# An attention and feed-forward block on one core: softmax rows turned in blocks of 32 on VectorE and carried by plain transfers, with the first rows, the second entry's blocks and the last rows in another order

## The chip, the cores and the metric

The kernel runs on one core of a Trainium2 chip. The metric is the device time of one execution in microseconds (us), given as the median of several runs. The profile is of one further execution. The engines are TensorE (PE for matmuls, PEld for weight loads), VectorE (DVE), ScalarE (ACT), GpSimd (POOL) and SyncE (SP), which here issues every transfer.

## What is computed

`x` has 2 entries of 1024 rows of 512. There are 16 heads of width 128, and the feed-forward part has 1365 hidden columns. Cut to what matters:

```python
xn = layernorm(x)
q, k, v = (einsum('bsd,hed->bhse', xn, W) for W in (W_Q, W_K, W_V))
scores = where(causal, -1e9, einsum('bhse,bhme->bhsm', q, k) / sqrt(128))
z = einsum('bhsm,bhme->bhse', softmax(scores), v)
x = x + layernorm(einsum('bhse,hde->bsd', z, W_O))
h1, h3 = (einsum('bsd,hd->bsh', layernorm(x), ternary(w)) for w in (w1, w3))
x = x + layernorm(einsum('bsh,dh->bsd', silu(h1) * h3, ternary(w2)))
```

`ternary(w)` rounds w/s to -1, 0 or 1 and multiplies by s, the mean of |w|.

## The kernel before

**Number forms.** A projection is made of three matmul products: a tensor is split into a lead and a low part and a difference of the two (`lead_and_low` L403, `difference_form` L412, for weights; `block_unit` L357 for x), in a 32-bit form[...]. `combine` (L423) puts the main and the difference product together. Scores (L522) and values (L584) are plain f32 matmuls, each of two instructions.

**Heads and steps.** N = 32 heads (16 for each of the two entries, b), two to a pair g. A head n has 8 rows i of 128 queries; row i has L = 128(i + 1) keys. `order` lists the 256 (n, i), and the loop at L683 takes one a step, idx. `scores(n, i)` (L517) does the row's matmuls into one of two `s_ps` buffers; DVE masks (L527) and takes the row maximum (L531), ACT makes exp and the row sum (L538), DVE inverts it (L543), ACT scales (L544). `look(idx + 3)` at step idx keeps the scores three rows ahead.

**Turning the softmax.** `values` needs the softmax with keys on the partitions. POOL copies the row's upper and lower 16-bit words apart (`half`, L549), SP issues one transposing transfer for the row (`halfT`, L554), and one step later `join` (L564) has DVE put the words together in `pt` (L570). Two rows share a `pt`, so a head has four pairs m, and `values(n, m)` (L575) multiplies 2m + 2 key tiles of 128x256. It runs where (idx - 3) is odd, for the pair that ended at idx - 3. ACT takes the result out twice (L593, L595), DVE and POOL make low and difference (L598, L601).

**What fills a step.** `put` gives steps of a head their extra matmul work: query and key projections of the next head (`query_key_unit` L432), values of the next pair of heads (`value_unit` L454), output projections of the last pair (`output_units` L478, each with two DVE operations L496 and L499 on `acc`). `side` holds small things by step: mean of |w|, statistics of the second entry, ternary weights (L187). Four `ps_m` buffers take the projection results.

**What sets the order.** A scheduler at compile time orders instructions in the order of the code and by readiness. `tc.issue_after(ins)` puts the instructions of a block behind `ins` on its own engine; `behind("max", "half", "exp", "turn")` (L508) does that with the last recorded row maximum (DVE), word copy (POOL), exp (ACT) and transposing transfer (SP). SP issues in order, and at most eight of its transfers are in flight, for they take turns on eight semaphores.

**First rows (L606 to L635).** x is loaded in eight tiles of 128 rows to `acc`, weights between. Statistics of rows 0 to 3 are taken, then `block_unit(0, t)` normalises on ACT (L366), transposes on PE (L375) and makes lead (ACT), low (DVE) and difference (POOL); rows 4 to 7's statistics are taken between. Queries and keys for the first 512 tokens follow, then the blocks of rows 4 to 7, queries and keys for the second 512, and then the loop at L677 with scores of three rows and four value units.

**Second entry's blocks (L705).** The eight `block_unit(1, t)` lie in steps 4 to 7 of head 14, each with its own load of x just ahead of its normalising.

**Last rows.** After the loop the last output units, values and join are mixed (L765 to L774). The feed-forward part then runs four blocks of 512 rows. In the last one `finish_last` (L833) does, for each row tile by itself: statistics from PSUM, root on ACT, three one-column DVE steps, output on ACT, the sum with `acc` on POOL (DVE for the last), and the store.

Of the kernel before, what the change touches and what calls it, by code (L numbers as in the profile page):

```python
# [28 lines left out]
P = 128  # L29
# [6 lines left out]
def sandwich_kernel(  # L36
# [67 lines left out]
    def row_stats(mv, src):  # L104
        st = small.tile([P, nc.vector.BN_STATS_DIM], FP, name="bnst")
        nc.vector.bn_stats(out=st, in_=src)  # L106
        nc.vector.bn_aggr(out=mv, in_=st)

# [209 lines left out]
    with ExitStack() as att:  # L318
        ppool = att.enter_context(tc.tile_pool(name="p", bufs=1))
        hpool = att.enter_context(tc.tile_pool(name="half", bufs=1))  # L320
        htpool = att.enter_context(tc.tile_pool(name="halfT", bufs=1))
# [9 lines left out]
        xs, r_in, shifts, lows_in, leads_in = {}, {}, {}, [], []  # L331
# [24 lines left out]

        def block_unit(b, t):  # L357
# [3 lines left out]
            if b == 0:  # L361
                src = xt = acc[:, t, :]
            else:
                src = xt = xpool.tile([P, D], FP, name="xt")
                nc.sync.dma_start(xt, x[b, ts(t, P), :])
            nc.scalar.activation(  # L366
                xt, src, AF.Identity, scale=r_in[b][:, t : t + 1],
                bias=shifts[b][:, t : t + 1],
            )
# [4 lines left out]
            for c in range(NC):  # L374
                nc.tensor.transpose(ps[:, c, :], xt[:, ts(c, P)], ident)  # L375
            lead, low, diff = (form[:, :, ts(tl, P)] for form in xs[b, k])
            leads_in.append(nc.scalar.mul(lead, ps, LEAD / T12).ins)  # L377
            lows_in.append(
                nc.vector.scalar_tensor_tensor(  # L379
                    low, lead, -T12, ps, ALU.mult, ALU.add  # L380
                ).ins
            )
            nc.gpsimd.tensor_tensor(diff, lead, low, ALU.subtract)
# [19 lines left out]
        def lead_and_low(kind, n, part):  # L403

            if (kind, n) not in weights:
                weights[kind, n] = [form(kind, "a"), form(kind, "l")]
            lead, low = (w[:, part] for w in weights[kind, n][:2])
            raw = wraw[kind, n][:, part]
            nc.scalar.mul(lead, raw, LEAD)
            nc.gpsimd.tensor_tensor(low, raw, lead, ALU.subtract)  # L410
# [21 lines left out]
        def query_key_unit(n, kind, k):  # L432
# [12 lines left out]
            for c in range(NC):  # L445
                nc.tensor.matmul(  # L446
                    diff, lhsT=forms[2][0][:, c, :], rhs=forms[2][1][:, c, :],
                    start=(c == 0), stop=(c == NC - 1),
                )
            combine(  # L450
                proj[n, kind, k], main, diff, SCALE if kind == 0 else 1.0
            )
# [64 lines left out]
        def scores(n, i):  # L517
# [27 lines left out]

            words = p_sb.bitcast(U16).rearrange("p (k two) -> p k two", two=2)
            half = hpool.tile([P, 2 * longest], U16, name=f"half{i % 2}")
            for k in range(2):
                copy = nc.gpsimd.tensor_copy(half[:, ds(k * L, L)], words[:, :L, k])  # L549
            marks["half"].append(copy.ins)  # L550
            halfT = htpool.tile(
                [P, 2 * (i % QT + QT + 1), P], U16, name=f"halfT{i % QT}"
            )
            turn = nc.sync.dma_start_transpose(  # L554
                halfT[:, 0 : 2 * (i + 1), :], half[:, : 2 * L]
            )
            marks["turn"].append(turn.ins)
            return halfT
# [5 lines left out]
        def join(n, i):  # L564
            turned = live.pop((n, i))
            m, il = divmod(i, 2)
            if il == 0:
                pts[n, m] = ptpool.tile([P, NT - 2 + 2 * (m % 2), KB], FP, name=f"pt{m % 2}")
            words = pts[n, m].bitcast(U16).rearrange("p t (q k) -> p k t q", k=2)
            nc.vector.tensor_copy(  # L570
                words[:, :, 0 : i + 1, ts(il, P)],
                turned[:, 0 : 2 * (i + 1), :].rearrange("p (k t) q -> p k t q", k=2),
            )

        def values(n, m):  # L575
# [5 lines left out]
            ps = ps_m.tile([P, TB], FP, name="mm")  # L581
            for kt in range(2 * m + 2):
                c0 = max(0, kt - 2 * m) * P
                nc.tensor.matmul(  # L584
                    ps[:, c0:KB],
                    lhsT=proj[g, 2][:, kt, ts(j, P)],
                    rhs=pts[n, m][:, kt, c0:KB],
                    start=(kt == 0),
                    stop=(kt == 2 * m + 1),
                )  # L590

            lead, low, diff = (w[:, ts(half, KB)] for w in zs[g, qb, j])
            nc.scalar.mul(lead, ps[:, :KB], LEAD / T12)  # L593
            copy = zpool.tile([P, KB], FP, name="zf", bufs=2)
            nc.scalar.copy(copy, ps[:, :KB])  # L595
# [12 lines left out]
        load_raw(0, 0)  # L608
        load_raw(1, 0)
        for t in range(QT, NT):  # L610
            stats_load(0, t)
        load_raw(2, 0)
        for t in range(NT):
            with ExitStack() as order:
                if t >= QT:
                    block_unit(0, t - QT)
                    order.enter_context(tc.issue_after(lows_in[t - QT]))
                row_stats(mv_in[0][:, t, :], acc[:, t, :])
                if t % 2 == 1:
                    std_unit(0, t - 1, 2)  # L620
            k = t - QT - 2
            if k >= 0:
                with tc.issue_after(lows_in[k + 1]), tc.issue_after(leads_in[k + 1]):
                    lead_and_low(k, 0, EVERY)
                    difference_form(k, 0, EVERY)
        for k in range(2):
            for t in range(QT, NT):
                if k == 1:
                    block_unit(0, t)
            for kind in range(2):  # L630
                query_key_unit(0, kind, k)
# [305 lines left out]
```

## Time and profile before

| | |
|---|---|
| median of 3 runs | 1545.23 us (1544.26 to 1546.73) |
| profiled execution, own time | 1546.35 us |
| its span | 1544.5 us |
| mean granted TensorE clock | 0.995 |
| instructions | 21108 |
| transfers by the first queue | 357512 packets, 163.62 MB, 47.2% of 16 engines |
| first matmul starts, last ends | 8.76 us, 1534.40 us |

The span is the time from the first to the last instruction that the profiler recorded; the execution's own time has 1.85 us around it. "Busy" counts an engine's instructions; a matmul's end is modelled, so PE's share is not its share of peak. A row of groups has line, engine, operation, tiles (written, then read), shapes and count, then busy us, mean ns of one, and idle time just ahead of them with what ended it. A row of waits has us in total, times and longest. Windows are counted from the start of the span.

### The profile page before, as it was taken

Reading aid. Unit: us, or ns where it says so; the run is one execution under the profiler, and the core shown is the slowest. Engines: PE = TensorE matmul, PEld = TensorE weight load, DVE = VectorE, ACT = ScalarE, POOL = GpSimd, SP = SyncE. Lnnn points to the kernel's source line nnn. Section 1 sums busy time; section 2 is a strip of 40 time slices with the busy share of each in tenths; the row PEclk is TensorE's granted clock in tenths of the full one; section 3 lists DMA queues with packets and bytes.
Section 4 is the critical chain, followed back from the end, with each engine's and each line's share of the span. In section 5 each row is a group of like instructions: output and inputs, shape, how many; then the busy total and the mean of one; then the engine's idle time right before and its main releaser. Section 6 shows DMA issues by size and latency. Waiting matters only on the chain.

```text
span 1544.5 us, 21108 instructions
## 1 busy us (share of the span) xinstructions
PE 1488.7 (96%) x7078; PEld 1188.7 (77%) x7078; DVE 1165.4 (75%) x2101; ACT 789.2 (51%) x1568; POOL 790.5 (51%) x861
## 2 busy tenths in 40 slices
PE   5999999999999999999999999999999999999997
PEld 4777878787878786876787877777878877788885
DVE  5678787878787879798888888888887786455343
ACT  4555545454556455556655555555555564344233
POOL 4465555555555667767766666666665441210010
PEclk9999999999999999999999999999999999999999
DMA  2465555555554456457655555555554457210000
GB/s 88 82 143 122 111 122 108 122 110 121 109 130 96 107 112 140 114 116 166 163 117 116 116 117 116 117 117 116 109 103 89 81 125 213 86 55 7 35 28 28
DMA packets 357622, 164.97 MB, mean 107 GB/s; under 512 B 311093, under 2 KB 324405, under 8 KB 357513
## 3 DMA queue, kind: packets, MB, share of 16 engines
q1 hardware_dynamic: 357512, 163.62, 47.2%
q8 instruction: 56, 0.92, 0.2%
q14 instruction: 54, 0.43, 0.1%
HBM read 73.39 MB, written 14.68 MB: 57 GB/s over the span
## 4 chain that ended last, share of the span: by engine, by line
PE 47%; DVE 4%; issue 1%; POOL 1%; ACT 1%; DMA 1%; SPq 0%; ACTq 0%; DVEq 0%; POOLq 0%
PE mm L298 10%; PE mm L584 8%; PE mm L441 6%; PE s_ps L522 6%; PE mm L465 5%; PE yp L806 5%; PE mm L485 4%; PE mm L446 3%; DVE pt L570 1%; DVE nm L531 1%; PE trx L238 0%; DVE bnst L106 0%; POOL half L549 0%; DVE raw L208 0%; POOL acc L266 0%
## 5 line engine op out<-in xcount | busy, mean ns | idle before, releaser
L549 POOL COPY half<-p_sb 128x640 uint16<-128x640 uint16 (+7 forms) x512 | 348.9, 711 | 436.7 <-issue 301.5
L538 ACT ACTIVATE p_sb<-s_ps,nm 128x128 f32<-128x128 f32 (+7 forms) x256 | 190.1, 743 | 351.0 <-DVE nm L531 328.7
L522 PE MATMUL s_ps<-k,q 128*128 128x512 f32 (+3 forms) x768 | 289.6, 486 | 1.9 <-ACT p_sb L538 1.8
L584 PE MATMUL mm<-pt,v_sb 128*128 128x256 f32 (+1 forms) x1280 | 271.6, 359 | 8.5 <-DVE acc L496 5.8
L584 PEld LDWEIGHTS mm<-pt,v_sb 128*128 128x128 f32 x1280 | 238.9, 190 | 51.5 <-DVE acc L496 13.3
L570 DVE COPY pt<-halfT 128x256 uint16<-128x256 uint16 (+7 forms) x256 | 272.6, 1065 | 0.5 <-DMA halfT<-half 0.5
L544 ACT ACTIVATE p_sb<-p_sb,ri 128x128 f32<-128x128 f32 (+7 forms) x256 | 198.4, 775 | 118.9 <-DVE ri L543 118.2
L531 DVE TENSOR_REDUCE nm<-s_ps 128x1 f32<-128x128 f32 (+7 forms) x256 | 193.2, 755 | 6.1
L601 POOL TENSOR_TENSOR zd<-za,zl 128x256 fp32r<-128x256 f32 x128 | 148.6, 1161 | 74.9 <-DVE zl L598 74.9
L522 PEld LDWEIGHTS s_ps<-k,q 128*128 128x128 f32 x768 | 130.6, 190 | 65.5 <-issue 54.7
L465 PE MATMUL mm<-va,xb 128*128 128x256 f32 x512 | 153.1, 299 | 2.2 <-DVE k L426 2.2
L527 DVE TENSOR_TENSOR s_ps<-s_ps,causal 128x128 f32<-128x128 f32 x256 | 75.0, 293 | 94.3 <-PE s_ps L522 93.2
L465 PE MATMUL mm<-vd,xb 128*128 128x256 f32 x512 | 144.7, 284 | 1.4 <-ACT k L424 1.4
L465 PE MATMUL mm<-vl,xb 128*128 128x256 f32 x512 | 144.4, 282 | 0.0
L441 PE MATMUL mm<-xb,qa 128*128 128x512 f32 x256 | 121.0, 473 | 1.4 <-ACT xb L377 1.4
L441 PE MATMUL mm<-xb,ka 128*128 128x512 f32 x256 | 113.1, 442 | 0.1
L441 PE MATMUL mm<-xb,ql 128*128 128x512 f32 x256 | 102.8, 402 | 2.5 <-DVE xb L379 2.5
L465 PEld LDWEIGHTS mm<-va,xb 128*128 128x128 f32 x512 | 97.7, 191 | 7.0 <-DVE k L426 2.6
L441 PE MATMUL mm<-xb,kl 128*128 128x512 f32 x256 | 101.9, 398 | 0.6 <-POOL kl L410 0.6
L465 PEld LDWEIGHTS mm<-vl,xb 128*128 128x128 f32 x512 | 97.8, 191 | 4.4 <-issue 2.4
L485 PE MATMUL mm<-oa,za 128*128 128x512 f32 x256 | 95.5, 454 | 4.8 <-DVE acc L496 3.5
L465 PEld LDWEIGHTS mm<-vd,xb 128*128 128x128 f32 x512 | 97.4, 191 | 2.2 <-ACT k L424 1.6
(150 smaller groups left out, 2815.8 us busy)
## 6 DMA issues: line engine op xcount, KB each, us to landing
wqk<-wq SPq DMA_DIRECT2D x32, 256.0 KB, 3.4
wqk<-wk SPq DMA_DIRECT2D x32, 256.0 KB, 3.6
wvo<-wv SPq DMA_DIRECT2D x16, 512.0 KB, 3.9
wvo<-wo SPq DMA_DIRECT2D x16, 512.0 KB, 3.8
xt<-x SPq DMA_DIRECT2D x32, 256.0 KB, 3.4
raw<-w SPq DMA_DIRECT2D x30, 256.0 KB, 3.4
tern<-raw SPq DMA_DIRECT2D x30, 256.0 KB, 2.7
xt<-w SPq DMA_DIRECT2D x24, 227.5 KB, 3.1
```

The lines of the kernel that those rows point to most:

```text
L298: nc.tensor.matmul(ps[:fl, :], lhsT=t[:, c, :], rhs=bl[k][:, c, :], start=(c == 0 and k == 0), stop=(c == NC - 1 and k == 1),)
L441: nc.tensor.matmul(main, lhsT=forms[f][0][:, c, :], rhs=forms[f][1][:, c, :], start=(c == 0 and f == 0), stop=(c == NC - 1 and f == 1),)
L465: nc.tensor.matmul((main, main, diff)[f][:, ts(t, 2 * P)], lhsT=forms[f][0][:, c, token], rhs=forms[f][1][:, c, :], start=(t == 0 and c == ...
L485: nc.tensor.matmul((main, main, diff)[f], lhsT=zs[g, t // QT, j][f][:, ts(t % QT, P)], rhs=weights[3, g][f][:, 2 * j : 2 * j + 2, :], star ...
L522: nc.tensor.matmul(s_ps[:, ds(k0, kl)], lhsT=proj[n, 0, i // QT][:, ts(i % QT, P)], rhs=proj[n, 1, k0 // TB][:, :kl], start=True, stop=True,)
L531: top = nc.vector.tensor_reduce(nm, s_ps[:, :L], axis=AX.X, op=ALU.max, negate=True)
L538: e = nc.scalar.activation(p_sb[:, :L], s_ps[:, :L], AF.Exp, bias=nm, accum_out=rs)
L544: nc.scalar.mul(p_sb[:, :L], p_sb[:, :L], ri)
L549: copy = nc.gpsimd.tensor_copy(half[:, ds(k * L, L)], words[:, :L, k])
L570: nc.vector.tensor_copy(words[:, :, 0 : i + 1, ts(il, P)], turned[:, 0 : 2 * (i + 1), :].rearrange("p (k t) q -> p k t q", k=2),)
L584: nc.tensor.matmul(ps[:, c0:KB], lhsT=proj[g, 2][:, kt, ts(j, P)], rhs=pts[n, m][:, kt, c0:KB], start=(kt == 0), stop=(kt == 2 * m + 1),)
L601: nc.gpsimd.tensor_tensor(diff, lead, low, ALU.subtract)
```

## The change

1. Softmax: a row goes from `scores` as it is. `turn(n, i)` has DVE transpose it in blocks of 32x32 into a tile `blocks`. The even row's missing key tile is cleared by POOL. When the odd row of a pair is done, SP issues 16 plain transfers, one for each source strip of 32 partitions and each destination strip, in runs of 64 words (256 B). `values` reads the last key tile and writes back in strips of 32. `half`, `halfT` and `join` go.
2. `turn(idx + 2)` is called at step idx, `values` at idx for the pair that ended at idx - 2, and output and value units lie in other steps.
3. The second entry's blocks lie one a step, from step 5 of head 14, with the load of x one step ahead.
4. First rows: a square root ahead of all; statistics and normalising in pairs of rows, odd rows normalised on DVE; wv loaded ahead of rows 4 to 7; first q and k leads on DVE; half of the differences on DVE; main products of q and k ahead of their difference products; value units between the second blocks and the queries and keys.
5. Last rows: all turned in the loop; `finish_last` works on pairs, with row 3 ahead of row 2 on DVE.

```diff
+    nc.scalar.activation(small.tile([P, 1], FP, name="root", bufs=1), eps, AF.Sqrt, bias=eps)
...
+        def block_load(b, t):
+            normal[b, t] = xt = xpool.tile([P, D], FP, name="xt")
+            nc.sync.dma_start(xt, x[b, ts(t, P), :])
+
+        def normal_unit(b, t):
+            if b == 0:
+                normal[b, t] = acc[:, t, :]
+            xt = normal[b, t]
+            if b == 0 and t % 2 == 1:
+                return normalise(xt, xt, mv_in[b], r_in[b], t)
+            return nc.scalar.activation(
+                xt, xt, AF.Identity, scale=r_in[b][:, t : t + 1],
+                bias=shifts[b][:, t : t + 1],
+            )
...
+            eng = nc.vector if b == 0 and tl >= QT // 2 else nc.gpsimd
...
-            words = p_sb.bitcast(U16).rearrange("p (k two) -> p k two", two=2)
-            half = hpool.tile([P, 2 * longest], U16, name=f"half{i % 2}")
-            for k in range(2):
-                copy = nc.gpsimd.tensor_copy(half[:, ds(k * L, L)], words[:, :L, k])
...
-            turn = nc.sync.dma_start_transpose(
-                halfT[:, 0 : 2 * (i + 1), :], half[:, : 2 * L]
-            )
...
+        def turn(n, i):
+            L = (i + 1) * P
+            p_sb = live.pop((n, i))
+            m, il = divmod(i, 2)
+            kts = 2 * m + 2
+            if il == 0:
+                blocks_of[n, m] = b = tpool.tile(
+                    [P, 4 * (NT - 2 + 2 * (m % 2)), 2, 32], FP, name=f"blocks{m % 2}"
+                )
+                clear = nc.gpsimd.memset(b[:, 4 * (kts - 1) : 4 * kts, 0, :], 0.0)
+                marks["half"] += 2 * [clear.ins]
+            b = blocks_of[n, m]
+            nc.vector.transpose(
+                b[:, 0 : 4 * (i + 1), il, :],
+                p_sb[:, :L].rearrange("p (b r) -> p b r", r=32),
+            )
+            if il == 0:
+                return
...
+            moved = b.rearrange("p (t b) i r -> p t b (i r)", b=4)
+            for to in range(4):
+                for of in range(4):
+                    move = nc.sync.dma_start(
+                        pt[ts(to, 32), 0:kts, ts(of, 64)], moved[ts(of, 32), 0:kts, to, :]
+                    )
+            marks["turn"] += 2 * [move.ins]
...
+        with past(*normal_pair(0)):
+            done = normal_pair(2)
+        with past(*done):
+            for kind in range(2):
+                lead_and_low(kind, 0, EVERY, first=True)
+            blocks = [block_unit(0, t) for t in range(QT)]
+        lead, low, diff = blocks[-1]
+        with past(diff):
+            for kind in range(2):
+                difference_form(kind, 0, EVERY)
+        for rest in [query_key_unit(0, kind, 0) for kind in range(2)]:
+            rest()
+        with past(lead, diff, blocks[1][2]):
+            for part in (FRONT, BACK):
+                lead_and_low(2, 0, part)
+                difference_form(2, 0, part)
+            done = normal_pair(4)
+            with past(*done):
+                normal_pair(6)
...
+        value_unit(0, 0)
+        for t in range(QT, NT):
+            block_unit(0, t)
+        value_unit(0, 1)
+        look(0)
+        for kind in range(2):
+            query_key_unit(0, kind, 1)()
+            look(1 + kind)
+            load_raw(kind, 1)
+        value_unit(0, 2)
+        for k in range(2):
+            turn(*order[k])
+        value_unit(0, 3)
...
-                put((0, 1, 1, 3, 5, 7, 7, 7), outs)
...
+                put((0, 0, 0, 2, 2, 4, 6, 6), outs)
...
-                if idx >= 3 and (idx - 3) % 2 == 1:
-                    rest = values((idx - 3) // NT, (idx - 3) % NT // 2)
+                if idx >= 2 and (idx - 2) % 2 == 1:
+                    rest = values((idx - 2) // NT, (idx - 2) % NT // 2)
...
-                if idx > 0:
+                if idx + 2 < len(order):
                     with behind("max"):
-                        join(*order[idx - 1])
+                        turn(*order[idx + 2])
...
+            for u in (t, t - 1) if t == QT - 1 else (t - 1, t):
+                y, yp, tt = last["y"][:, u, :], yps[b, tb][u], tb * QT + u
+                ua, ushift = last["a"][:, u : u + 1], last["shift"][:, u : u + 1]
+                if u == QT - 1:
+                    nc.vector.tensor_scalar(y, yp, ua, ushift, ALU.mult, ALU.add)
+                else:
+                    nc.scalar.activation(y, yp, AF.Identity, scale=ua, bias=ushift)
+                eng = nc.vector if u >= QT // 2 else nc.gpsimd
+                eng.tensor_tensor(y, y, acc[:, tt, :], ALU.add)
+                nc.sync.dma_start(out[b, ts(tt, P), :], y)
```

## The prediction

> **What bounds the kernel now.** I read the page's busy shares first, then its chain and its costliest groups, then the windows of 50 us and of 5 us, PE's waits, and last SP's own queue, since the change puts 2048 transfers on it.
>
> ```profile
> PE 1488.7 (96%) x7078; PEld 1188.7 (77%) x7078; DVE 1165.4 (75%) x2101; ACT 789.2 (51%) x1568; POOL 790.5 (51%) x861
> PE 47%; DVE 4%; issue 1%; POOL 1%; ACT 1%; DMA 1%; SPq 0%; ACTq 0%; DVEq 0%; POOLq 0%
> L549 POOL COPY half<-p_sb 128x640 uint16<-128x640 uint16 (+7 forms) x512 | 348.9, 711 | 436.7 <-issue 301.5
> L570 DVE COPY pt<-halfT 128x256 uint16<-128x256 uint16 (+7 forms) x256 | 272.6, 1065 | 0.5 <-DMA halfT<-half 0.5
> L531 DVE TENSOR_REDUCE nm<-s_ps 128x1 f32<-128x128 f32 (+7 forms) x256 | 193.2, 755 | 6.1
> ```
>
> PE bounds: it is idle for 1544.5 - 1488.7 = 55.8 us in all, and the change removes no matmul. So the work taken from POOL (L549) and DVE (L570) is worth only what it frees of those 55.8 us. The windows say where they lie (time, PE, PEld, DVE, ACT, POOL, clock, DMA share, GB/s):
>
> ```profile
> 0.00:50.00 50.00, 33.75 (x155) 27.08 (x156) 24.88 (x51) 22.23 (x41) 18.80 (x26) 0.93 0.23 78
> 600.00:650.00 50.00, 46.31 (x230) 36.24 (x230) 42.09 (x70) 30.31 (x60) 38.23 (x36) 1.00 0.59 138
> 700.00:750.00 50.00, 43.43 (x223) 34.09 (x222) 43.13 (x87) 33.16 (x60) 37.38 (x37) 1.00 0.75 186
> 1500.00:1550.00 50.00, 34.40 (x152) 27.52 (x150) 15.38 (x33) 13.40 (x21) 3.70 (x3) 0.92 0.06 21
> ```
>
> 16.3 us are idle in the first 50, 2.1 in the next 50, 22.2 over 100 to 1250 (summed over those windows; 3.7 and 6.6 in the two shown), 5.2 over 1250 to 1350, 10.1 behind the last matmul. PE's waits in the middle are nearly all for DVE:
>
> ```profile
> PE mm L584 <- DVE acc L496: 5.8, 8, 0.8
> PE mm L485 <- DVE acc L496: 3.5, 4, 1.3
> PE mm L446 <- DVE q L428: 2.8, 2, 1.5
> ```
>
> At the start there is a loss beside idle time. From 17.7 to 22.4 us the 128x512 matmuls start 0.43 us apart, later 0.23; from 30 to 39.6 again 0.43, with a granted clock of 0.69 and 0.66 in the rows 30:35 and 35:40. Those are about 11 and 18 matmuls at 0.2 us extra.
>
> **SP's queue, the resource that the change loads.** SP's timeline (start, us from first to last end):
>
> ```profile
> 0.72 1.82 SPq L335 DMA_DIRECT2D acc<-x  x4
> 3.53 1.89 SPq L335 DMA_DIRECT2D acc<-x  x4
> 576.40 0.57 SPq L213 DMA_DIRECT2D tern<-raw  x1
> 577.02 0.42 SPq L193 DMA_DIRECT2D raw<-w  x1
> 577.56 0.49 SPq L396 DMA_DIRECT2D wqk<-wk  x1
> ```
>
> A plain transfer issues in 0.43 us, and back to back the starts lie 0.46 to 0.48 us apart, 0.51 where it waits for one eight places earlier (4.48 to 5.00 us). L193 is the nearest in shape (512 pieces of 512 B): its own issue is 0.42, the next starts 0.54 after it.
>
> **The change, part by part.** It is summed against the profiled execution: 1546.35 us, span 1544.5, so 1.85 around it; the median shown, 1545.23, is 1.1 less.
>
> *Removed:* 512 POOL copies (348.9 us), 256 joins on DVE (272.6 us), 256 transposing transfers on SP (median issue 1.33 us, 341 us). None is on PE's path: at their ends PE waited 2.4 us for pt.
>
> *Added on DVE:* 256 block transposes of 128xL f32. No row shows one. Nearest is L531, the same 256 shapes read once: 0.755 us, 193 us; the upper end is the joins' own 1.065. Less than nothing is excluded, since they read every element. I take 0.755: DVE falls by 80 us, to 70%. On POOL 128 clears of 128x128 at 0.20 us (the ident memset at 0.71 us): 26 us, hidden, POOL being near 30%. These clears and the transposes now wait for moves that still read the blocks. Behind them on DVE stand the next mask and row maximum, for which ACT's exp and then PE wait. A block buffer comes round three steps after its moves were queued, 3 x 4.8 = 14.5 us; the moves need 16 x 0.5 + 3 = 11 us. Covered; every us beyond stands on PE's path.
>
> *Added on SP:* 128 pairs x 16 moves. With 0.47 to 0.54 us each a pair costs 7.6 to 8.6 us, and some 230 other transfers in the attention add 0.9. A pair has two steps: (1283 - 45)/128 = 9.67 us before, 9.6 with the gain below. So SP goes to 88 to 99%. I take 0.49, 91%: the plain back-to-back rows, since a move has 64 to 256 pieces, fewer than L193. The pair's moves are queued four steps (19 us) ahead of the matmuls that read them; they need 11. Below nothing: SP saves its 341 us of transposes, but nobody waited for SP, so no gain.
>
> *On the DMA engines:* 327,680 pieces of 256 B, 20,480 an engine. The packet records have 294,912 packets of 256 B (those of the transposes) at 22.8 ns in the mean and 10,240 plain ones of 512 B at 33.7. At 22.8 the pieces take 467 us an engine, at 33.7 690; with 250 us for the rest that is 58 to 76% of the 1229 us of attention. The Trainium skill speaks against it: "DMA: Bandwidth & Descriptors", section "Specifications", gives 512 B as the least size for line rate, with a read-modify-write below. If that doubled a packet of 33.7 ns, the pieces alone would take 1380 us, more than the stage, and the kernel would end near 1930 us. The same page, "Rules for kernel authors", puts a plain rearranging DMA at 19 times the hardware transpose: 19 x 3.6 us, the median landing of a transpose, is 68 us a row where a step has 4.8. I go with the rows. The trace moved 256 B packets as fast per packet as any, and here each run of 64 words is contiguous at both ends, the rearranging within 32 being DVE's.
>
> *Reads in strips of 32:* the last key tile's matmul has 128 columns as before (0.274 us) and ACT's two copies 256 (0.374, 0.367). If strips doubled ACT's, 256 x 0.37 = 95 us more put ACT at 57%: hidden, at nothing.
>
> *The middle.* values come a step earlier and the output units are spread over even steps; up to three still share a step. DVE, behind which PE waits, loses 0.31 us a step. Of 22.2 us idle I take 9 as gained; bounds 0 and 15. The second entry's x loads go one step earlier but on odd steps stand behind 16 moves (8 us, then 3.4 to land, against 4.8): ACT's normalising waits, exp and then PE behind it. Before, PE lost about 4 us there; I take the same, with 8 more as the upper end. Loads for normalising after attention meet the moves too: +2.
>
> *The start.* The early square root takes the table load (1.28 us at 5.47) into the wait for x (first statistics at 3.68). Two rows' statistics end at 5.4, root, reciprocal and shift at 6.2, the first transposes near 7.1 instead of 8.76. Rows 2 and 3 follow at 9.2; then DVE makes qa and ka (0.6 each, to 11.0) and four lows (0.69 each, to 13.8). The second matmul, which sat idle until low at 17.55, can go at 13.8: -3.7. From there 24 matmuls, at first slow, as before. Then the second half, 25.2 to 40.5 us: its 16 transposes and 24 matmuls are 7.2 us at full pace and two scores 0.3; the other 7.8 are 3.7 of idle on ACT, DVE and POOL and the slow clock. Value units (24 x 0.12 = 2.9 us each) now stand between; I leave 1.5 us: -6.3. DVE also has four rows' statistics and value forms in that stretch, so of -10 I take -8; bounds -4 and -11. Cover gone, each form that comes late costs its 0.7 to 1.3 us. wv goes ahead of rows 4 to 7 on SP (1.5 us later), needed only at 15 us.
>
> *The ends.* Of 5.2 us at 1250 to 1350 I take 1.5, as the last rows are turned two steps earlier. Behind the last matmul (1534.4) the last row's root waited on ACT to 1537.42 behind three outputs, and two tiny DVE steps took 0.74 and 1.18 beside POOL; its output issued at 1541.5. Now statistics end at 1535.4, root behind two outputs at 1536.6, three small steps to 1537.1, DVE 0.7 + 0.7, the other row's sum to 1539.3: -2.2, less POOL's interference, -2 (bounds 0 and -3).
>
> Sum: -8 - 9 + 2 - 1.5 - 2 = -18.5; on the median 1526.7, say 1527.
>
> **The rivals.**
> (1) SP becomes the bound. For: the 0.54 behind the many-piece transfer; only eight transfers are in flight. Against: 0.43 to 0.48 for plain ones. 2048 + 234 = 2282 issues fill 1229 us at 0.539 us each; above 0.547 the gain is used up, and it is slower. At 0.555 it costs 1266.5 - 1229 = 37.5: 1565 us.
> (2) The middle keeps its waits: the 22.2 us are the output units' turns, not DVE's load. Then only start and ends count, about -10: 1535.
> (3) The DMA engines bind by the 512 B rule: 1700 us or more. Against: the packet rows.
> (4) The change doesn't do what it says, the starts staying serial on DVE: part of (2), 1540 to 1546.
>
> **How the numbers follow.** Forecast 0.55 (1515 to 1538), rival (2) with (4) 0.16, of which 0.05 within 0.2%, rival (1) 0.25 (0.02 within), (3) 0.04. About 0.2% is what a measurement of this kernel can tell from no change. Faster 0.66, same 0.07, slower 0.27. The range 1513 to 1570 leaves out the worse half of (1), (3) and a small low tail; the forecast's own is 1515 to 1538.
>
> **What would show it.** Right: SP's move issues near 0.49 us with gaps between pairs; the DVE transpose near 0.75; PE idle in 100 to 1250 near 13; 128x512 matmuls at 0.23 us by 22 us; last output issued near 1539. Wrong: PE waiting for DMA pt, DVE's transpose waiting for DMA, SP's moves without gaps, 256 B packets over 40 ns.

## The result, and the profile after

The changed kernel takes 1865.7 us (median of 4 runs, 1865.4 to 1872.1) against 1544.7 before, measured again beside it: a ratio of 1.209, with an interval of 1.206 to 1.212. The forecast was 1527, its range 1513 to 1570; the result lies on the side of rival (1), at a price that rival (1) did not reach. The profiled execution took 1865.4 us, its span is 1863.6.

The page's busy shares, its chain, the group of block transposes and the largest moves (in the last line, the number is the time from issue to landing):

```profile
PE 1597.3 (86%) x7078; PEld 1233.2 (66%) x7078; DVE 1136.5 (61%) x2107; ACT 773.1 (41%) x1556; POOL 398.5 (21%) x472
...
SPq 40%; PE 28%; DMA 9%; issue 8%; DVE 8%; ACT 4%; POOL 3%; DVEq 0%; POOLq 0%; ACTq 0%
SPq L596 38%; PE mm L301 7%; PE mm L454 4%; DMA pt<-blocks 4%; PE yp L862 4%; PE s_ps L539 3%; PE mm L616 3%; PE mm L482 2%; PE mm L461 2%; PE mm L502 2%; ACT p_sb L555 1%; DVE blocks L584 1%; DVE acc L513 1%; DVE nm L548 1%; DMA raw<-w 1%
...
L584 DVE STREAM_TRANSPOSE blocks<-p_sb 128x128 f32<-128x128 f32 (+7 forms) x256 | 188.1, 760 | 78.6 <-DMA pt<-blocks 77.7
...
pt<-blocks SPq DMA_DIRECT2D x512, 64.0 KB, 2.2
```

The bound has moved. The chain that was PE's for 47% and SP's for 0% is now SP's for 40%, nearly all of it line 596, the moves. Every engine is less busy by share than before; nothing but SP's queue is full. The tile's own view gives least, median and most of one move's issue, and SP's timeline shows them in a row (start, us from first start to last end):

```profile
L596 SPq DMA_DIRECT2D pt<-blocks x2048: 585/601/1922, 38.2 to 1606.6; - x187
```

```profile
603.48 10.18 SPq L596 DMA_DIRECT2D pt<-blocks  x16
613.70 0.58 SPq L406 DMA_DIRECT2D wvo<-wv  x1
614.45 10.47 SPq L596 DMA_DIRECT2D pt<-blocks  x16
625.03 0.53 SPq L216 DMA_DIRECT2D tern<-raw  x1
625.60 0.43 SPq L196 DMA_DIRECT2D raw<-w  x1
```

Sixteen moves take 10.2 to 10.5 us, 0.64 to 0.66 a start. With the other transfers between, these pairs start 11.0 and 11.7 us apart (11.7 is also the median over the trace's records), where PE needs 9.6. There is no gap here: the next pair's moves are ready before SP is. The moves that carry 16 KB have nearly the same issue time as those that carry 64 KB (medians 0.595 to 0.609 us, worked out from the trace's records for the four sizes), so it is the count that costs.

Summed over the trace's records, SP's stretch with moves runs from 38.2 to 1607.2 us and holds 2282 transfers, as counted in the forecast. Their issues take 1379.3 us, the short gaps between them (under 0.3 us each) 121.9, together 1501.2 us or 0.658 us each; longer idle time is 67.8 us, of which 43 lie in 700 to 870. The forecast gave that stretch 1229 us. So 1501 - 1229 = 272 us is the price of an issue, and 68 is SP itself waiting. 1527 + 272 + 68 = 1867, against 1865.7 measured. This is bookkeeping, since SP's stretch is counted whole: that it closes says that the start and the ends came near the forecast. The experiments below test the causes.

What waits now, in the waits of the changed kernel (us in total, times, longest):

```profile
POOL blocks L581 <- DMA pt<-blocks: 434.7, 114, 12.1
ACT p_sb L555 <- DVE blocks L584: 363.3, 103, 9.4
...
PE mm L616 <- DMA pt<-blocks: 68.8, 30, 4.9
PE s_ps L539 <- ACT p_sb L555: 46.8, 31, 5.7
```

POOL's clears and DVE's transposes wait until moves have read the blocks, exp waits until a transpose has read its row, PE waits for exp and for the moves. The whole row hangs on SP from both sides.

The 68 us of idle SP is a second loss. In the stretch of the second entry's blocks the windows show PE at 69% of the time (time, PE, PEld, DVE, ACT, POOL, clock, DMA share, GB/s) and SP's timeline a period of 21 to 23 us for a pair:

```profile
700.00:870.00 170.00, 116.94 (x485) 88.98 (x484) 89.07 (x164) 62.79 (x123) 45.15 (x46) 0.84 0.37 87
```

```profile
755.67 10.18 SPq L596 DMA_DIRECT2D pt<-blocks  x16
765.94 1.01 SPq L363 DMA_DIRECT2D xt<-x  x2
767.00 0.42 SPq L406 DMA_DIRECT2D wvo<-wo  x1
778.30 10.25 SPq L596 DMA_DIRECT2D pt<-blocks  x16
```

The chain of waits in this stretch tells why SP stands still from 767.4 to 778.3, a stall that is as long as the moves themselves:

```profile
765.94 2.85 DMA xt<-x
768.82 0.82 ACT xt L371
769.69 1.11 PE tr L386 x4
770.80 4.18 PE mm L482 x24
774.98 3.26 PE mm L616 x16
```

The load of x (line 363) is queued behind the pair's 16 moves. ACT's normalising waits for it, PE's transposes wait for that, and the matmuls behind them on PE (value units, then the values whose end sets `pt` free) wait for PE. Only then can the next 16 moves start. It is a closed loop: moves, load, normalising, PE, moves.

### The profile page after: what moved, and what is told of

It reads as the page before. It is cut to its first block, busy times and chain, and to the rows that moved or that the text cites. A ratio compares the mean times of both kernels' runs of the same rounds, so it can differ in the third digit from the quotient of the medians.

```text
span 1863.6 us, 23761 instructions
## 1 busy us (share of the span) xinstructions
PE 1597.3 (86%) x7078; PEld 1233.2 (66%) x7078; DVE 1136.5 (61%) x2107; ACT 773.1 (41%) x1556; POOL 398.5 (21%) x472
## 4 chain that ended last, share of the span: by engine, by line
SPq 40%; PE 28%; DMA 9%; issue 8%; DVE 8%; ACT 4%; POOL 3%; DVEq 0%; POOLq 0%; ACTq 0%
SPq L596 38%; PE mm L301 7%; PE mm L454 4%; DMA pt<-blocks 4%; PE yp L862 4%; PE s_ps L539 3%; PE mm L616 3%; PE mm L482 2%; PE mm L461 2%; PE mm L502 2%; ACT p_sb L555 1%; DVE blocks L584 1%; DVE acc L513 1%; DVE nm L548 1%; DMA raw<-w 1%
## 5 line engine op out<-in xcount | busy, mean ns | idle before, releaser
L555 ACT ACTIVATE p_sb<-s_ps,nm 128x128 f32<-128x128 f32 (+7 forms) x256 | 188.5, 738 | 481.0 <-DVE blocks L584 363.3
L616 PE MATMUL mm<-pt,v_sb 128*128 128x256 f32 (+1 forms) x1280 | 294.9, 380 | 81.3 <-DMA pt<-blocks 68.8
L616 PEld LDWEIGHTS mm<-pt,v_sb 128*128 128x128 f32 x1280 | 252.7, 202 | 156.8 <-issue 94.2
L539 PE MATMUL s_ps<-k,q 128*128 128x512 f32 (+3 forms) x768 | 304.1, 517 | 48.3 <-ACT p_sb L555 46.8
L584 DVE STREAM_TRANSPOSE blocks<-p_sb 128x128 f32<-128x128 f32 (+7 forms) x256 | 188.1, 760 | 78.6 <-DMA pt<-blocks 77.7
L539 PEld LDWEIGHTS s_ps<-k,q 128*128 128x128 f32 x768 | 138.6, 198 | 136.5 <-issue 58.8
L636 POOL TENSOR_TENSOR zd<-za,zl 128x256 fp32r<-128x256 f32 x128 | 94.7, 740 | 471.3 <-DVE zl L633 435.2
L633 DVE SCALAR_TENSOR_TENSOR zl<-za,zf 128x256 fp32r<-128x256 f32 x128 | 68.6, 536 | 88.5 <-ACT zf L628 88.5
L581 POOL MEMSET blocks<- 128x128 f32 x128 | 26.1, 204 | 441.2 <-DMA pt<-blocks 434.7
L502 PE MATMUL mm<-od,zd 128*128 128x512 f32 x256 | 84.5, 411 | 39.5 <-ACT zf L628 37.8
L454 PE MATMUL mm<-xb,ql 128*128 128x512 f32 x256 | 113.9, 445 | 0.0
```

The source lines that it names most:

```text
L454: nc.tensor.matmul(main, lhsT=forms[f][0][:, c, :], rhs=forms[f][1][:, c, :], start=(c == 0 and f == 0), stop=(c == NC - 1 and f == 1),)
L502: nc.tensor.matmul((main, main, diff)[f], lhsT=zs[g, t // QT, j][f][:, ts(t % QT, P)], rhs=weights[3, g][f][:, 2 * j : 2 * j + 2, :], star ...
L539: nc.tensor.matmul(s_ps[:, ds(k0, kl)], lhsT=proj[n, 0, i // QT][:, ts(i % QT, P)], rhs=proj[n, 1, k0 // TB][:, :kl], start=True, stop=True,)
L555: e = nc.scalar.activation(p_sb[:, :L], s_ps[:, :L], AF.Exp, bias=nm, accum_out=rs)
L584: nc.vector.transpose(b[:, 0 : 4 * (i + 1), il, :], p_sb[:, :L].rearrange("p (b r) -> p b r", r=32),)
L616: nc.tensor.matmul(dst, lhsT=proj[g, 2][:, kt, ts(j, P)], rhs=rhs, start=(kt == 0), stop=(kt == 2 * m + 1),)
```

## The experiments

**What sets the price of a pair: the count of moves (first runs).** Two kernels were run beside the changed one: one with eight moves a pair, each of 128 words in place of 64, one with only the loads put ahead. The eight moves read the blocks of the first 64 partitions only, each twice, and leave out the rest, so they don't carry the whole softmax; they move the same number of bytes.

```diff
# eight moves (twice as wide)
-                for of in range(4):
+                for of in range(2):
-                        pt[ts(to, 32), 0:kts, ts(of, 64)], moved[ts(of, 32), 0:kts, to, :]
+                        pt[ts(to, 32), 0:kts, ts(of, P)], moved[ts(of, 32), 0:kts, ts(to % 2, P)]
# loads first: the load of x is queued on SP ahead of the step's moves
-            side[block_at - 1 + t].append(lambda t=t: block_load(1, t))
+            early[block_at - 1 + t] = t
...
+                if idx in early:
+                    block_load(1, early[idx])
                 if idx + 2 < len(order):
                     with behind("max"):
                         turn(*order[idx + 2])
```

> The changed kernel with 8 moves a pair instead of 16, each of 128-word runs instead of 64: the same bytes, half the issues; it fills pt with the right amount of data from the wrong strips, so the softmax is scrambled. Theory A (SP's issue of a move, 0.60 us and 0.04 between two, is the bound whatever the move's size): a pair falls from 16 x 0.64 + 0.95 = 11.2 to 6.1 us, below the 9.5 that PE needs, so PE is the bound again and the rest of the change shows: 1520 to 1540 us. Theory B (the bytes through the DMA engines, or the landing of a pair's data): the same bytes, so it stays above 1750 us.

Measured 1569.9 us (ratio 1.016, 1.014 to 1.018). B is out, for the same bytes move 296 us faster, and one move of twice the bytes issues in the same time (ns, least, median, most):

```profile
L596 SPq DMA_DIRECT2D pt<-blocks x1024: 585/601/1899, 37.9 to 1309.1; - x171
```

The packets change too (163,840 of 512 B in place of 327,680 of 256 B), but the time that they take, summed over the records, falls only from 449 to about 408 us an engine, so the DMA engines don't explain 296. Theory A's mechanism holds; its figure was missed by 30 us. Those are not the middle: PE's idle time is 6.4 us over 100 to 600, but 25.8 over 600 to 720, the blocks' loop. The chain is PE's again, for 80%.

> The changed kernel with the second entry's eight loads of x put on SP ahead of the step's moves instead of behind them. Theory A with a closed loop there (moves, then the load behind them, then ACT's normalising, PE's transpose and values, which free pt for the next moves: 22 us a pair against 11.2): four pairs lose about 10 us less each, 1866 to about 1825. Rival (the sum of SP's issues alone sets the time): no change, within 5 us of 1866.

Measured 1841.0 us (1.191, 1.189 to 1.194), 25 less than the changed kernel. PE's busy time in 700 to 870 rises from 116.94 to 134.30 us. The loop was real; it was worth 25 and not 40, since elsewhere SP stays the bound.

> Eight moves a pair (scrambled softmax, as in the run with eight moves) and the second entry's loads of x ahead of the moves. With eight moves alone PE was idle 25.8 us between 600 and 720, where the blocks lie, and 6.4 us in the 500 before that. Theory A (issue count plus the closed loop at the blocks, nothing else): that idle falls to about 4, so 1570 - 25 = 1535 to 1545 us, level with or just below before; then DVE's and POOL's relief by itself has won nothing in the middle, and the gain is the start's. Rival (relief of DVE wins 9 us in the middle as I had forecast): 1527 us.

Measured 1544.5 us (1.000, 0.9996 to 1.0013). The four kernels make a table:

| | load behind the moves | load ahead |
|---|---|---|
| 16 moves | 1865.7 | 1841.0 |
| 8 moves | 1569.9 | 1544.5 |

Each row differs by 25 us, each column by 296. Both causes add up, and neither needs the other. PE's idle time over 600 to 720 fell to 9.2 us, not to 4. But 1544.5 is also no gain at all, although SP and the loads are out of the way; of that below.

**What a move costs, by itself.** A kernel that computes nothing of the block and only issues transfers of one size (64 KB) in several forms.

> The move measured by itself: series of transfers back to back of one form each, nothing else computed (the output is a copy of x). From SP, 32 partitions: the move as it is; with the destination in one run; with the source in one run; both in one run; the same from HBM in pieces and in one run; to HBM in pieces; then 128 partitions within SBUF in pieces and in one run; the move from ACT's and from POOL's queue. Theory A1 (having SBUF on both sides costs it): 0.60 us for all within SBUF, 0.43 with HBM on one side. Theory A2 (pieces on both sides, so three dimensions, cost it): 0.60 for the forms in pieces, 0.43 for one run. Theory A3 (32 partitions cost it): 0.60 for all of 32, 0.43 for 128. Theory A4 (the kernel around it costs it, its waits or its other traffic): 0.43 for the move here.

SP's timeline: `tb` has one run at the target and pieces at the source, `td` one run at both ends, all within SBUF; `tf` comes from a tensor in HBM in pieces, `tg` from it in one run; `away` goes there in pieces.

```profile
44.97 10.38 SPq L44 DMA_DIRECT2D tb<-src  x16
...
65.94 10.06 SPq L53 DMA_DIRECT2D td<-src  x16
...
85.79 9.08 SPq L66 DMA_DIRECT2D tf<-home  x14
94.97 7.50 SPq L69 DMA_DIRECT2D tg<-home  x16
102.52 10.41 SPq L78 DMA_DIRECT2D away<-src  x16
```

A transfer within SBUF issues in 0.59 to 0.61 us (starts 0.63 to 0.65 apart) whether its runs are broken or whole. One from HBM in one run issues in 0.42 (0.46 apart), one from HBM or to HBM in pieces in 0.607. So the surrounding kernel adds nothing (A4 is out), and the 32 partitions don't either (A3 is out: 128 partitions within SBUF took 0.605 in one run and 0.715 in pieces). Neither A1 nor A2 holds by itself: HBM on one side is not cheap in pieces, and one run is not cheap within SBUF. From POOL's queue the same move takes 0.58. The plain rows that the forecast went by were all loads from HBM. What exactly lifts 0.42 to 0.60 isn't settled: line 193 of the kernel before also loads pieces from HBM and issued in 0.43 at the median, and its stores from SBUF took from 0.33 to 0.59, shown further below.

**Is it the count, or another order of instructions?** The scheduler at compile time orders by readiness, so a change of transfers also changes TensorE's order (4% of the 7078 matmuls between 16 and 8 moves). Five kernels, of which two follow here, tie every TensorE instruction behind the one before it in the code; in their traces all 7078 matmuls stand in one and the same order.

```diff
+    def on_pe(op, *args, **named):
+        if held.get("pe") is None:
+            r = op(*args, **named)
+        else:
+            with tc.issue_after(held["pe"]):
+                r = op(*args, **named)
+        held["pe"] = r.ins
+        return r
```

> The changed kernel with loads first (1841.0), with every TensorE instruction tied behind the one before it in the code, so that its order is that of the code. Theory A: SP's issuing sets the time, whatever TensorE's order: 1830 to 1850. Rival O: a part of the loss was TensorE's order: under 1800.

> The run with eight moves of 128 words and loads first (1544.5; it scrambles the softmax's order, the bytes are the same), with TensorE's order tied in the same way, so that it is that of the run beside it with 16 moves. Theory A: 16 against 8 moves costs 272 to 300 us in one and the same order, so this is 1535 to 1565. Rival O: the difference falls under 250 us, this being 1580 or more or the other under 1800.

Measured 1847.1 (1.197, 1.195 to 1.199) and 1556.8 us (1.008, 1.007 to 1.010). With the order the same, 16 against 8 moves costs 290 us. Theory A stands, and the order is no part of this difference; tying by itself cost 6 us with 16 moves and 12 with eight.

**The parts of the change without the turning.** The kernel before, with the change's first rows and last rows, all else as it was; then with the second entry's blocks one a step as well, the load behind the transposing transfer or ahead of it.

```diff
# start and ends: the change's part 4, and its finish_last, on the kernel before
# spread, on top:
-                put((4, 5, 5, 6, 6, 6, 7, 7), units)
+                    put(
+                        2 * [(block_at + t) % NT],
+                        [lambda t=t: normal_unit(1, t), lambda t=t: block_unit(1, t)],
+                    )
```

> The kernel before with the new first rows and the new last rows alone; the softmax is turned as before. The changed kernel's own trace lost about 9 us less in its first 32 us and 0.4 us less behind its last matmul. If that carries through: 1545 - 9 = 1536 us. Rival (what the start gains is waited away again when the first rows' softmax is late): within 2 us of 1545.

Measured 1534.4 us (0.993, 0.991 to 0.995), the one version that beats both kernels: about 10 us less.

> The old turning with the new first and last rows (1534.4 us) and the second entry's blocks one a step with the load a step ahead, as the change has them. SP has only one transposing transfer of 1.3 us a step, so the load isn't late: of some 4 us idle at the blocks 2 to 4 are won, 1531 us. Rival (ACT and DVE are as loaded there, the units only lie elsewhere): 1534 us, no change.

Measured 1556.2 us (1.007, 1.006 to 1.009), 22 above the last; both theories missed. ACT's normalising waited 10.4 us for x between 560 and 720.

> The kernel before with the new start and ends and with the second entry's blocks one a step, as in the spread run, but each x load queued on SP ahead of the step's transposing transfer and not behind it. Theory L: the 22 us that the spread run lost came from its late loads (ACT's normalising waited 10.4 us for x in 560 to 720, and PE behind it). Then most comes back: 1534 to 1545, PE busy over 600 to 720 at 110 or more (114.3 without the spread, 102.6 with it). Rival P: one normalising, four transposes and a block's three forms in every step cost by themselves, wherever the load stands: 1550 to 1556, PE busy near 103.

Measured 1545.3 us (1.000, 0.999 to 1.001), against 1534.4: half of the 22 was the late load, half is the spread itself. The windows of the three kernels, in this order, for 600 to 720:

```profile
600.00:720.00 120.00, 114.30 (x557) 89.86 (x557) 105.47 (x191) 68.79 (x139) 83.67 (x85) 1.00 0.57 135
```

```profile
600.00:720.00 120.00, 102.55 (x466) 78.13 (x466) 87.65 (x155) 55.24 (x112) 63.08 (x67) 0.93 0.49 112
```

```profile
600.00:720.00 120.00, 111.15 (x534) 87.73 (x533) 97.08 (x176) 62.98 (x128) 74.12 (x77) 0.97 0.50 117
```

PE's idle time goes from 5.7 to 17.5 and back to 8.9 us, and the granted clock goes with it (1.00, 0.93, 0.97). The whole spans show what that adds: the second kernel's is 24.1 us longer than the first's, and 11.9 of them are not idle time but the same 7078 matmuls taking longer (1495.1 us busy against 1483.2).

**The order of values and units.** On the start-and-ends kernel, values a step earlier and the changed places of the output and value units (the cut shows the first two).

```diff
-                if idx >= 3 and (idx - 3) % 2 == 1:
+                if idx >= 2 and (idx - 2) % 2 == 1:
-                put((0, 1, 1, 3, 5, 7, 7, 7), outs)
+                put((0, 0, 0, 2, 2, 4, 6, 6), outs)
```

> The kernel before with the new start and ends, and with the changed order of the fill: values for the pair that ended two steps ago (before three), output units at steps 0,0,0,2,2,4,6,6 and value units at 0,2,6,7. Turning and the second entry's blocks as before. Theory U: this order is what the middle lost in the run with eight moves and loads first (about 10 us of idle more than before): 1540 to 1545, PE's idle time over 100 to 600 and 720 to 1250 up by 5 to 10 us. Rival: it is neutral or gives what was forecast of the middle (up to 9 us): 1525 to 1535.

Measured 1633.7 us (1.057, 1.056 to 1.059), which neither had. PE waited 36.1 us for DVE's joins (pt, 26 times) and 50.0 for exp ahead of scores. Of the 7078 matmuls in the trace, 1,352 stand elsewhere in the order than in the kernel it was built on. Without an earlier turn the values lack a step of lead; how much is that and how much the order was not told apart, so this run says nothing of the units alone.

**A way out: two queues.** The changed kernel with loads first, with some of the 16 moves issued by POOL.

```diff
-                    move = nc.sync.dma_start(
+                    eng = nc.gpsimd if (4 * to + of) % 8 in (1, 3, 6) else nc.sync
+                    step = eng.dma_start(
```

> The changed kernel with its right data, 10 of a pair's 16 moves from SP and 6 from POOL's queue, and the second entry's loads ahead of the moves. Theory A (SP's issues bound it): SP has 10 x 0.64 + 0.95 = 7.4 us a pair, POOL 6 x 0.58 = 3.5, both below 9.5, so PE is the bound: 1535 to 1550 us. Theory B (16 transfers a pair are too many for the engines or their semaphores whatever the queue): above 1700 us.

Measured 1660.8 us (1.076, 1.074 to 1.078): neither. SP has gaps again, but PE is idle for 2 to 6 us of every 50 between 100 and 500. POOL's moves also travel in other packets: by the records 12,288 of 1 to 4 KB replace 122,880 of 256 B, so these kernels change more than who issues.

> The changed kernel with loads first, its 16 moves split 13 on SP and 3 on POOL (10 and 6 in the run with two queues, 1660.8). Theory Q: in that run POOL's 3.4 us of issuing a pair held up its clears and differences, and with them DVE and ACT; SP alone at 13 needs 13 x 0.64 + 0.95 = 9.3 us a pair against 9.6, so with POOL's part halved: 1545 to 1600. Rival S: the pair's length is set by how long the moves take from the last transpose to the last landing, and SP's share sets that: longer than with 10 and 6, 1660 to 1720.

Measured 1714.6 us (1.110, 1.108 to 1.112): in rival S's range; more on SP is worse even where its sum is under a pair's time. The order was the scheduler's own here, so this run alone does not show the cause.

> The run with two queues (10 moves on SP, 6 on POOL, loads first, 1660.8) with one block buffer for each of the four pairs of a head, where two took turns. Theory C: with the queues no longer the bound, the buffers are: the transposes of a pair wait until the moves of the pair before last have read its blocks, so that transposes, moves and landings form a round that is longer than two pairs. With four buffers this wait is gone: 1545 to 1590, and SP's wait for DVE's blocks (171 us there) falls. Rival D: POOL's order (its six moves stand between its clears and differences) or the moves' late landing holds the rows up, and the buffers don't matter: 1640 to 1665.

> The changed kernel with loads first (all 16 moves on SP, 1841.0) with the same four block buffers. Theory A: SP's issuing alone sets the pair (16 x 0.64 + about 0.95 = 11.2 us), and buffers don't touch it: 1825 to 1845. Rival C: also here the round of two block buffers sets it (POOL's clears waited 435 us for moves in the changed kernel): 1700 or less.

```diff
-                    [P, 4 * (NT - 2 + 2 * (m % 2)), 2, 32], FP, name=f"blocks{m % 2}"
+                    [P, 4 * kts, 2, 32], FP, name=f"blocks{m}"
```

Measured 1704.8 (1.104) and 1896.4 us (1.227), slower by 44 and 55 than with two buffers. All four theories missed. With more buffers the scheduler chose another order (370 and 466 of the 7078 matmuls stand elsewhere than in the kernels that they were built on), and with 16 moves TensorE's wait for exp ahead of scores rose from 49.9 to 150.6 us. The next two take the order out for the two queues; four buffers with all 16 moves on SP were not run in the tied order, so there the order as the cause is argued, not shown.

> The run with 10 moves on SP and 6 on POOL (1660.8), with TensorE's order tied in the same way. Theory O: its loss against eight moves (116 us) came of the order that the scheduler chose (TensorE waited 44.5 us for exp ahead of scores and 26.7 for the forms of z): 1545 to 1580. Rival Q: the queues do it (POOL's issues between its clears and differences, SP's 7.5 us a pair and landings): 1640 to 1670.

> The run with two queues and four block buffers (1704.8), with TensorE's order tied in the same way. Theory O: the buffers made it slower only by way of the order (459 rows differ), so tied it is no slower than the two buffers tied, and 1545 to 1580. Rival C or Q: two buffers tied stay at 1640 or more, and then this tells whether the buffers' round is why (well below the two buffers) or POOL's queue (the same as with two).

Measured 1583.7 (1.026, 1.024 to 1.028) and 1584.8 us (1.027, 1.025 to 1.028). PE's waits with two queues, first in the scheduler's order, then tied (line 57 is the helper):

```profile
PE s_ps L539 <- ACT p_sb L555: 44.5, 31, 3.0
PE mm L502 <- ACT zf L631: 26.7, 14, 3.3
```

```profile
PE s_ps L57 <- ACT p_sb L566: 1.6, 2, 1.1
PE mm L57 <- ACT zf L642: 1.5, 1, 1.5
```

Theory O came out 4 us above its range. The run with two queues had lost 116 us against eight moves; tying TensorE's order took 77 off it, and against eight moves in the same order 27 are left. With the order fixed the block buffers make no difference (1583.7 and 1584.8), so theory C falls: not the buffers' round, as I had it, but the order was behind the 44 us.

> The two-queue run in the tied TensorE order (10 on SP, 6 on POOL, 1583.7) with 12 moves on SP and 4 on POOL. SP then needs 12 x 0.644 + 0.95 = 8.7 us of a pair's 9.6. Theory S: what is left over eight moves (27 us) comes of SP's share, its later landings and the loads behind them: 1590 to 1620. Rival Q: it comes of POOL's issues, which stand between its clears and differences: 1557 to 1580.

Measured 1626.1 us (1.054, 1.052 to 1.056): on theory S's side, 6 us above its range. In the tied order 10, 12 and 16 moves on SP give 1584, 1626 and 1847 us. SP's share costs time before it is full, by 21 us a move from 10 to 12 and 55 from 12 to 16. By which path it does so at 10 and 12 was not followed.

> The kernel before with the new start and ends (1534.4), with TensorE's order tied to that of the code in heads 1 to 12 and 18 to 28 only (48 of some 8,270 rows differ). Theory O: the order of code is the better one here too, as it was for the moves (idle of 3.8 us over 100 to 600 with eight moves tied, 6.6 in this kernel untied): 1529 to 1534. Rival: the scheduler's order suits this turning, and tied it waits: 1534 to 1550.

Measured 1551.0 us (1.005, 1.003 to 1.006): the rival, one us above its range. For the turning of before, the scheduler's order is the better one, by 17 us.

## Why the prediction was wrong, point by point

**The step that failed: "I take 0.49, 91%: the plain back-to-back rows, since a move has 64 to 256 pieces, fewer than L193."** A move issues in 0.60 us, and the starts lie 0.64 apart. That makes 10.3 us of a pair's moves where 8 were reckoned, and 0.658 us for each of the 2282 transfers, far above the 0.547 from which rival (1) decides. So the cost of an issue was mis-sized, and with it the bound: SP was taken at 91% and was full. Two things went wrong in choosing the row. It was the row nearest in pieces, when pieces are not what counts: 64 and 256 of them cost nearly the same. And the rows taken were loads from HBM, and among the cheaper ones. No plain transfer within SBUF stood in the trace before, and its plain transfers differ from line to line:

```profile
L213 SPq DMA_DIRECT2D tern<-raw x33: 567/588/844, 518.6 to 1150.8; - x33
L831 SPq DMA_DIRECT2D out<-y x12: 332/338/338, 1367.4 to 1493.1; - x12
L142 SPq DMA_DIRECT2D xt<-w x35: 564/859/1496, 61.6 to 377.1; - x35
```

The first two are stores from SBUF to HBM, the third is a load from HBM. The sentence "A plain transfer issues in 0.43 us" was therefore wrong as a reading of that trace: summed over its records, the 234 plain transfers of the attention took 0.58 us in the mean and 0.53 at the median. The trace had no row for the move and gave no ground to leave 0.60 out, so the bounds, 0.47 to 0.54, were too narrow.

**Rival (1)** named the mechanism and its point of decision rightly, and its formula, fed with 0.658, gives the 272 us. It was given 0.25, and its size 1565.

**"The pair's moves are queued four steps ahead ... they need 11. Covered"**: with SP full they are not, and exp, transposes and clears wait as listed above. That is the consequence of the first step and not another cause: with eight moves and loads first POOL's clears wait 12.3 us for moves where they waited 434.7, exp 41.1 for the transposes where it waited 363.3, and PE's wait for moves is no longer on the list.

**The second entry's loads: "I take the same, with 8 more as the upper end."** The place was right, the size not: 25 us (table above) where nothing was added and 8 more at most were reckoned, since the load closes a loop with the moves. That loads stand behind 16 moves was seen; that the next moves stand behind the load, by way of PE's order, was not. The spread of the blocks, which had no price of its own, costs another 11 us on the turning of before.

**The middle: "Of 22.2 us idle I take 9 as gained."** No run shows it. With eight moves and loads first, DVE and POOL are relieved as forecast, and PE's idle time over 100 to 600 is 6.1 us where it was 4.7 before; with TensorE tied it is 3.8. Over 720 to 1250 it is 15.4 against 11.5. So the relief is worth about a microsecond at best, as rival (2) had it, and the ten that the start gains are given back between 600 and 1350: beside the start-and-ends kernel, eight moves with loads first have 3.4 us less of busy PE in 600 to 720, 4.8 in 720 to 1250 and 2.7 in 1250 to 1350.

**The start: -8.** About right: the start-and-ends kernel is 10 us faster, and the tail's share of that is under one. In the changed kernel the first matmul starts at 7.2 us where 7.1 was forecast, PE is busy for 39.1 of the first 50 us where it was 33.75, and the slow clock of 30 to 40 us is gone:

```profile
30.00:35.00 5.00, 4.31 (x21) 3.33 (x20) 3.60 (x8) 2.17 (x4) 0.00 (x0) 1.00 0.00 0
35.00:40.00 5.00, 5.00 (x30) 4.21 (x29) 3.59 (x10) 3.37 (x9) 0.00 (x0) 1.00 0.33 108
```

**The tail: -2.** Measured 9.7 us behind the last matmul, where it was 10.1: -0.4. The stretch is the timeline's last, of the changed kernel:

```profile
1856.30 2.93 POOL L916 TENSOR_TENSOR y<-y,acc 128x512 f32<-128x512 f32 x2 [43.69 <-ACT y L914]
1856.89 2.88 DVE L916 TENSOR_TENSOR y<-y,acc 128x512 f32<-128x512 f32 x2
```

Two sums on DVE beside two on POOL take 1.44 us each, not 0.7, and give back what the pairing saved.

**Right:** the block transpose, 0.755 forecast and 0.760 measured. DVE's share, 70%, came out in the kernel with eight moves and loads first. The 256-byte packets: the records give 21.9 ns in the mean for 327,680 of them, against 34.6 for the plain ones of 512 B. A byte costs more in the smaller packet, but nothing is doubled, so taking the rows was right, and the rule of the Trainium skill ("DMA: Bandwidth & Descriptors", section "Specifications") did not bind: no read-modify-write shows in these packets, and the page's own section "Why small descriptors are slow (HBM only)" excepts transfers within SBUF. The landing, 1.8 to 2.2 us a move at the median, and the eight in flight bind nothing: eight issues take 5.1 us. The 19 times of the same page's "Rules for kernel authors" did not show either: the packets of the moves take 449 us an engine, those of the transposing transfers took 421. The rule to weigh stood in the same table: it advises to coalesce many small transfers, those under 64 KB being mostly overhead. The moves have 16 to 64 KB, and halving their number at the same bytes was worth 290 us.

## What to carry to other kernels

Price a transfer by its issues before its bytes, and take the issue from a row with the same source and the same target; where the trace has none, measure the form by itself. Here it was 0.42 us out of HBM in one run and 0.60 within SBUF, from 16 to 64 KB alike, so that sixteen moves a pair cannot be paid where two transfers did. A queue's sum that comes out near 90% is not a cover but a rival that decides, and each load that stands in the same queue has to be followed until it meets that queue again. Where a scheduler orders the instructions, hold the order fixed before crediting a change of buffers or queues with a time.

## What the runs showed of the hardware that was not expected

A transfer within SBUF takes SP 0.59 to 0.61 us to issue: in one run or in pieces when measured by itself, and at 16 as at 64 KB in the kernel. A load from HBM in one run took 0.42 there. POOL issues the same move in 0.58 (0.565 to 0.567 in the kernels with two queues). Where TensorE idled more, its granted clock was lower: 0.84 over 700 to 870 of the changed kernel, where PE was busy for 69% of the time, and 1.00 over 100 to 600 of the start-and-ends kernel, where it was for 99%. Over the whole kernels the same 7078 matmuls were busy for 1597.3 us in the changed one, at a mean granted clock of 0.939, and for 1488.7 before, at 0.995, so a third of the 319 us between the spans is not idle time of PE but slower matmuls.
